# A four-layer graph network on one Trainium2 core: weights loaded ahead, split operands kept per tile, first messages inside the last convolution chunk, result loads together

## The chip, the core and the metric

The kernel runs on one core of a Trainium2 chip. The core has a matrix engine (TensorE, PE in the profile, with its weight loads listed as PEld), a vector engine (VectorE, DVE), an activation engine (ScalarE, ACT), a general engine (GpSimd, POOL) and a queue engine that mostly issues transfers (SyncE, SP). Each engine works through its own queue in order, and an instruction waits on semaphores for what other engines or transfers must have done. The sixteen DMA engines are shared by all queues. The metric is the device time of one execution in microseconds (us), taken as the median of three runs.

## The reference, cut to what matters

There are 8 graphs of 2048 nodes with 64 features and one adjacency matrix `adj` of 2048 x 2048 (zeros and ones, mostly zeros). Four layers follow each other, each in the form x = x + layer(relu(layernorm(x))). The change touches the end of layer 0, layers 1 and 2, and the end of layer 3.

```python
# layer 1, h = relu(layernorm(x)), K = 3 terms, D = 16 embedding dimensions
w = einsum('nd,dkio->nkio', embedding, weight);  b = embedding @ bias
x_g = [h, A @ h, 2 * A @ (A @ h) - h]
x = x + einsum('bnki,nkio->bno', x_g, w) + b
# layer 2, v = relu(layernorm(x)) with node 0 set to intervention_value
for _ in range(3):
    v = relu(concat(v, A @ v) @ W1.T + b1) @ W2.T + b2
x = x + v
# layer 3: attention of each node over its neighbours
x = x + softmax(adj * leaky_relu(e_src + e_dst)) @ (h @ weight) + bias
```

## The kernel before

**Layout.** Activations are kept as four pairs of graphs: for pair q a tile has 128 partitions (2 graphs x 64 features) and 2048 columns (nodes). Work along the nodes runs in four chunks of 512 columns (`ch`), or sixteen tiles of 128 nodes (`t` or `m`). Products with `adj` need the operand with the nodes on the partitions. Most large buffers are ten slots, `q0` to `q9`, of 16 KB per partition each, which the layers use again under other names.

**Product with the adjacency.** `adj_product` (L289) runs over the chunks, and in each over the sixteen tiles m. L300 loads a piece of `adj` transposed on SP (two tiles, 512 KB, with step=2), L312 rounds each tile on ACT to the reduced-precision format that the fast matmul takes, and eight matmuls follow (L153, all matmuls carry this line): four pairs times two halves of the operand, into `pp0` to `pp3`. To keep precision the operand is split into a rounded part `hi` (ACT, L219) and a rest `lo` (DVE, L220). `Split` holds these as four big buffers, `q6` to `q9`, each with eight node tiles. `first` runs ahead of a chunk's product, `after` behind each tile m, `done` at the chunk's end.

**End of layer 0.** `mix` (L608) works on the residual of layer 0 chunk by chunk, with its buffers `mix0` to `mix2` and `tanh` in `q6` to `q9`; with the norm it writes the operand of layer 1 (L618).

**Layer 1** (L1238). `by_node` transposes all node tiles (L1252) and splits them into `h_n`; a first product gives A h, and each chunk is transposed back into `ah`. Then `ah` is split into `ah_n`, the weights `wk` are loaded in six transfers (L1288, L1292) and adjusted by three DVE operations (L1295, L1296), the bias comes in two (L1300), and a second product runs. At the end of each of its chunks, `done2` loads the embedding (L1334, two transfers of 1 MB) and the residual (L1344), and runs the convolution: for each pair, four groups of eight matmuls into PSUM banks `pk`, sixteen multiplications (DVE, L1373), fourteen additions (POOL, L1378), and a fold (`po`, L1321). [...] The folds and the chunk's norm are put in a list, `waiting`, that `some` pops one at a time, during the next pair or the next chunk's product.

**Layer 2** (L1396). Three small weights are loaded (`block_diag`, L171 and L173) and combined by a few matmuls (`w2n`, `later`, `b1`). `messages(0, ...)` multiplies v by a weight for all sixteen tiles (`pn`), copies the result to `u`, and `u` is split into `u_n`. Three steps follow, each with one product; the chunk's own part is put into `pp` first (four matmuls). During the first steps `neighbours` finds, on POOL and DVE, the neighbours of each node for layer 3.

**Layer 3** gathers rows of neighbours on POOL (L1991), sums them and scatters the result to `att_rows` in DRAM (L2002). `result` (L2173) ends the kernel: for each chunk it loads x (L2178), for each of four tiles loads `att_rows` (L2182), transposes (L2185), adds (DVE, L2187), and stores four pieces (L2191), all transfers on SP.

**Order.** The program is recorded in the order of the source; a scheduler then sets the order in each engine's queue, within the dependences. A pool laid on memory that another pool has left waits for that memory tile by tile.

Of the kernel before, what the change touches and what calls it, by code (L numbers as in the profile page):

```python
# [7 lines left out]
F = mybir.dt.float32  # L8
# [11 lines left out]
P = 128  # L20
# [85 lines left out]
class Split:  # L106


    def __init__(self, slots, name, tags=("q6", "q7", "q8", "q9")):
        self.hi = Halves(slots, f"{name}_hi", tags[:2], True)  # L110
        self.lo = Halves(slots, f"{name}_lo", tags[2:], True)
        self.parts = self.hi, self.lo


class Kernel:
# [173 lines left out]
    def adj_product(self, src, w, ps, done, each=None, first=None, after=None, bufs=4, step=2):  # L289

        nc = self.nc
        for ch in range(NC):
            out = [ps.tile([P, CW], F, name=f"pp{q}", tag=f"pp{q}") for q in range(NP)]
            if first is not None:
                first(ch, out)
            for g in range(NT // step):
                at = w.tile([P, step, CW], F, name="adj_t", bufs=bufs)
                nc.sync.dma_start(  # L300
                    at,
                    self.a["adjT"][g * step * P : (g + 1) * step * P, ch * CW : (ch + 1) * CW]
                    .rearrange("(t p) n -> p t n", p=P),
                )
                for i in range(step):
                    m = g * step + i
                    if each is not None:
                        each(ch, m, at[:, i])
                    moving = at[:, i]
                    if self.short:  # L310
                        moving = w.tile([P, CW], F12, name="adj_12", bufs=bufs)
                        nc.scalar.copy(moving, at[:, i])  # L312
                    for j, part in enumerate(src.parts):
                        for q in range(NP):
                            self.mm(
                                out[q], self.exact(part(m)[:, q * P : (q + 1) * P]),
                                moving,
                                start=first is None and m == 0 and j == 0,
                                stop=m == NT - 1 and j == 1,
                            )  # L320
                    if after is not None:
                        after(ch, m, moving)
            done(ch, out)
# [282 lines left out]
    def mix(self, slots, ind, g, fcw, av, each=None):  # L606
# [4 lines left out]
        ring = slots.tile([P, 4, 2, CW], F, name="tanh", tag="q9")  # L611
        xe, xo = self.chebyshev(slots)
# [8 lines left out]
        with (  # L621
# [9 lines left out]
            for ch in range(NC):  # L631
                s = slice(ch * CW, (ch + 1) * CW)
                x, sq, xr = (b[:, ch % 2] for b in big)
# [604 lines left out]
    def layer1(self, slots):  # L1238
        nc, tc, a = self.nc, self.tc, self.a
        xe, xo = self.chebyshev(slots)  # L1240
        h_n = Split(slots, "h_n")
        ah = Halves(slots, "ah", ("q4", "q5"), True)
        lo, hi = slice(0, D), slice(D, P)
        ident = self.ident

# [9 lines left out]
        with (  # L1255
# [17 lines left out]
            self.adj_product(h_n, w, ps, done)  # L1273
        ah_n = Split(slots, "ah_n")
# [3 lines left out]
        with (  # L1278
            tc.tile_pool(reuse_waits="tile", name="k1", bufs=1) as k,
# [3 lines left out]
            DO = DE * D  # L1283
            w01 = []
            for i, order in enumerate(((0, 1), (1, 0))):
                t = k.tile([P, DO], F, name=f"w01_{i}")
                for j, kk in enumerate(order):
                    nc.sync.dma_start(t[j * D : (j + 1) * D], a["wk"][kk])  # L1288
                w01.append(t)
            w2 = k.tile([P, DO], F, name="w2")  # L1290
            for j in range(2):
                nc.sync.dma_start(w2[j * D : (j + 1) * D], a["wk"][2])  # L1292

            for t, h in zip(w01, (lo, hi)):
                nc.vector.tensor_sub(t[h], t[h], w2[h])  # L1295
            nc.vector.tensor_scalar_mul(w2, w2, 2.0)  # L1296

            bias = k.tile([P, NBLK], F, name="bias")
            for j in range(2):
                nc.sync.dma_start(  # L1300
                    bias[j * D : (j + 1) * D],
                    a["bias1"].rearrange("(b j) o -> j o b", j=2)[j],
                )

            fold = k.tile([P, D], F, name="fold")
            nc.vector.tensor_add(fold, ident[:, lo], ident[:, hi])
# [21 lines left out]
            def done2(ch, out):  # L1328
                while waiting:
                    some()  # L1330
                s = slice(ch * CW, (ch + 1) * CW)
# [16 lines left out]
                for q in range(NP):  # L1348
# [32 lines left out]
                    waiting.append(lambda q=q, accs=accs: fold_up(x, q, accs))  # L1381
# [9 lines left out]
            self.adj_product(ah_n, w, ps, done2, after=some, bufs=3)  # L1391
            while waiting:
                some()


    def layer2(self, slots):  # L1396
# [4 lines left out]
        with (  # L1401
# [5 lines left out]
            w1v = self.block_diag(k, a["W1T"][:D], "w1v")  # L1407
            w1e = self.block_diag(k, a["W1T"][D:], "w1e")
            w2 = self.block_diag(k, a["W2T"], "w2")

            w2n = k.tile([P, P], F, name="w2n")
            pw = ps2.tile([P, NP, P], F, name="pn")
            nc.tensor.transpose(pw[:, 0], w2, self.ident)
            nc.vector.tensor_copy(w2n, pw[:, 0])
            pw = ps2.tile([P, NP, P], F, name="pn")
            self.mm(pw[:, 0], w2n, w1v)
            self.mm(pw[:, 1], w2n, w1e)
            self.mm(pw[:, 2], self.col("b2").to_broadcast([P, P]), w1e)
            self.mm(pw[:, 3, :1], w1v, self.col("b2"))
            later = k.tile([P, 3, P], F, name="later")  # L1420
            nc.vector.tensor_copy(later, pw[:, :3])
            b1 = k.tile([P, 1], F, name="b1")
            nc.vector.tensor_add(b1, pw[:, 3, :1], self.col("b1"))
            own = [w1v, later[:, 0], later[:, 0]]
            seen = [w1e, later[:, 1], later[:, 1]]
            bias = [self.col("b1"), b1, b1]
            full = [P, NP, P]
            for q in range(NP):
                nc.vector.tensor_copy(v(q)[:, 0:1], self.col("iv"))

            def messages(step, tiles):

                for t in tiles:
# [4 lines left out]
                    if step == 0:  # L1438
                        self.copy(to, pn)
                    else:  # L1440
                        nc.vector.tensor_add(to, pn, later[:, 2].unsqueeze(1).to_broadcast(full))
# [12 lines left out]
            messages(0, range(NT))  # L1454
            for step in range(3):
# [3 lines left out]
                u_n = Split(slots, "u_n")  # L1459
                for t in range(NT):  # L1460
                    self.split(u_n, t, u(t))
# [88 lines left out]
    def layer3_near(self, slots):  # L1550
# [6 lines left out]
        with (  # L1557
# [8 lines left out]
            for _ in range(12):  # L1566
                next(first)
            for part in others:
# [299 lines left out]

class Scores:
# [73 lines left out]
class Near:  # L1943
# [5 lines left out]
    def __init__(self, kern, slots, w, ps):  # L1949
# [4 lines left out]
        self.x = slots.tile([P, 2, NP, CW], F, name="x_end", tag="q2")  # L1954
# [218 lines left out]
    def result(self):  # L2173

        nc, w, kern = self.nc, self.w, self.kern
        for ch in range(NC):
            x = self.x[:, ch % 2]
            nc.sync.dma_start(x, kern.xs[3][ch])  # L2178
            for i in range(TC):
                t = ch * TC + i  # L2180
                r = self.att(t)
                nc.sync.dma_start(r, kern.att_rows[t * P : (t + 1) * P])  # L2182
# [7 lines left out]
            for q in range(NP):  # L2190
                nc.sync.dma_start(kern.a["out"][q, :, ch * CW : (ch + 1) * CW], x[:, q])  # L2191


def kernel(tc, a):
    with ExitStack() as ctx:
        kern = Kernel(tc, ctx, a)
        with (
# [11 lines left out]
            def rest(short):  # L2209
                kern.short = short  # L2210
                with tc.tile_pool(reuse_waits="tile", name=f"taken{int(short)}", bufs=1) as slots.pool:
# [4 lines left out]
                    kern.layer1(slots)  # L2216
                    kern.layer2(slots)
# [71 lines left out]
```

## Time and profile before

| | |
|---|---|
| time, median of three runs | 2193.83 us (2192.85 to 2193.92) |
| the profiled execution's own time | 2206.33 us |
| its span, first to last instruction | 2204.5 us |
| PE busy | 1961.8 us, 89% of the span |
| DVE busy | 1135.3 us, 52% |
| ACT, POOL busy | 713.0 and 709.2 us, 32% each |
| bytes moved by DMA | 253.66 MB, mean 115 GB/s |
| loads of `adj` transposed, 512 KB each | 160, 4.0 us median from issue to landing |
| loads of `adj` transposed, 256 KB each | 64, 3.1 us |
| embedding, residual of layer 1 (1 MB each) | 11.8 us, 4.9 us |

Times in the profile are us from the span's start. A record of the timeline gives start, busy time, engine, line, operation, output and input, the number of records, and in brackets how long the engine was idle before and what released it. A float32 matmul leaves two records for one instruction; those of the products leave one.

### The profile page before, as it was taken

To read this page: it belongs to the slowest core of one execution; us is meant where nothing else is said; L and a number is where in the kernel's file an instruction comes from. 1 tells how busy PE (TensorE), PEld (TensorE's weight loads), DVE (VectorE), ACT (ScalarE), POOL (GpSimd) and SP (SyncE) were. 2 spreads that over 40 slices of the span, in tenths; PEclk is the share of its full clock that TensorE was granted. 3 is DMA by queue.
4 is the path that set the end of the run, shared out by engine and by line. 5 is a ranking of instruction groups with operands and counts; after the bars stand their busy time and mean duration, and the time that the engine had idled before them with its cause. 6 is when DMAs were issued, how large, how long until landed. Compare 5 with 4: busy or idle time off the path is not lost.

```text
span 2204.5 us, 21222 instructions
## 1 busy us (share of the span) xinstructions
PE 1961.8 (89%) x7461; PEld 1166.3 (53%) x7466; DVE 1135.3 (52%) x1964; ACT 713.0 (32%) x1351; POOL 709.2 (32%) x595
## 2 busy tenths in 40 slices
PE   5869999978879979999999998999999999679883
PEld 1426766632237755353443533777777666345432
DVE  7877677725651133525434245898602222349772
ACT  6422555524543341020110201434334333257300
POOL 0000467754310004707447173011000000278760
PEclk8868999977759989999999998999999999789986
DMA  8230233431124361050220402356433443465655
GB/s 317 75 107 22 90 112 115 129 129 57 39 77 120 118 159 53 0 153 1 76 77 10 106 1 77 118 192 219 154 123 124 144 144 125 143 189 169 185 152 203
DMA packets 108286, 253.66 MB, mean 115 GB/s; under 512 B 20400, under 2 KB 20544, under 8 KB 100864
## 3 DMA queue, kind: packets, MB, share of 16 engines
q1 hardware_dynamic: 91056, 185.64, 26.7%
q0 software_dynamic: 17104, 66.47, 9.9%
q8 instruction: 63, 1.03, 0.2%
q14 instruction: 63, 0.52, 0.1%
HBM read 218.30 MB, written 33.78 MB: 114 GB/s over the span
## 4 chain that ended last, share of the span: by engine, by line
PE 55%; DVE 11%; POOL 7%; issue 6%; DMA 5%; ACT 3%; SPq 1%; POOLq 0%; DVEq 0%; ACTq 0%
PE pp L153 23%; PE pk L153 16%; PE bank L153 4%; PE acc L153 3%; POOL ring L1991 2%; PE p L153 2%; PE pn L153 2%; DMA q<-in_adj_dram,order 1%; POOL q L1826 1%; DVE q L1841 1%; POOL dt L644 1%; DVE top L1532 1%; PE pd L153 1%; PE po L153 1%; PE pt L1252 1%
## 5 line engine op out<-in xcount | busy, mean ns | idle before, releaser
L312 ACT CAST adj<-adj_t 128x512 fp32r<-128x512 f32 x384 | 236.9, 619 | 724.2 <-PE pp L153 633.6
L1378 POOL TENSOR_TENSOR acc<-acc,y 128x512 f32<-128x512 f32 x224 | 277.4, 1269 | 451.7 <-DVE y L1373 451.7
L153 PE MATMUL pk<-q,w 128*128 128x512 f32 (+1 forms) x1024 | 358.1, 612 | 12.7 <-DVE w L1295 11.7
L153 PEld LDWEIGHTS pk<-q,w 128*128 128x128 f32 (+1 forms) x1024 | 136.6, 188 | 230.3 <-issue 182.5
L153 PE MATMUL acc<-q,ident 128*128 128x512 f32 x416 | 206.3, 623 | 28.9 <-DVE q L2081 17.1
L1373 DVE SCALAR_TENSOR_TENSOR y<-pk,bias,q 128x512 f32<-128x512 f32 x224 | 157.7, 746 | 138.0 <-PE pk L153 128.1
L153 PE MATMUL pp<-adj,u_n_hi 128*128 128x512 f32 x768 | 217.6, 402 | 0.0
L153 PE MATMUL pp<-adj,u_n_lo 128*128 128x512 f32 x768 | 214.7, 399 | 0.0
L153 PEld LDWEIGHTS pp<-adj,u_n_hi 128*128 128x128 f32 x768 | 143.9, 189 | 38.6 <-issue 5.4
L153 PEld LDWEIGHTS pp<-adj,u_n_lo 128*128 128x128 f32 x768 | 145.1, 189 | 34.8
L1991 POOL DMA_INDIRECT ring<-f_rows,near x121 | 140.2, 1159 | 67.9 <-issue 28.0
L153 PEld LDWEIGHTS acc<-q,ident 128*128 128x128 f32 x416 | 77.8, 197 | 106.6 <-issue 50.9
L2095 POOL IOTA q<- 128x2048 int32 x1 | 1.8, 1836 | 318.6 <-PE p L153 318.6
L1373 DVE SCALAR_TENSOR_TENSOR acc<-pk,bias,q 128x512 f32<-128x512 f32 x32 | 22.6, 746 | 144.9 <-PE pk L153 144.9
L153 PE MATMUL pp<-adj,x_ind_hi 128*128 128x512 f32 x256 | 94.7, 486 | 2.2 <-DVE q L722 1.9
L1826 POOL TENSOR_TENSOR q<-q,beta 128x512 f32<-128x512 f32 x57 | 68.0, 1194 | 54.5 <-DVE beta L1802 30.8
L153 PE MATMUL bank<-std,from_rows 32*128 32x512 f32 x128 | 47.5, 936 | 41.9 <-DVE std L260 33.8
L153 PE MATMUL pp<-adj,h_n_hi 128*128 128x512 f32 x256 | 79.4, 423 | 0.0
L1518 POOL DMA_INDIRECT q<-in_adj_dram,order x15 | 21.9, 1459 | 174.9 <-DVE top L1532 136.0
L153 PE MATMUL pp<-adj,h_n_lo 128*128 128x512 f32 x256 | 76.7, 413 | 0.0
L2062 DVE TENSOR_TENSOR q<-ring,e 128x1024 f32<-128x1024 f32 x58 | 70.1, 1220 | 11.5 <-PE acc L153 11.3
L153 PE MATMUL pp<-adj,ah_n_hi 128*128 128x512 f32 x256 | 73.8, 408 | 0.8 <-ACT adj L312 0.8
(416 smaller groups left out, 3179.0 us busy)
## 6 DMA issues: line engine op xcount, KB each, us to landing
adj_t<-in_adjT_dram SPq DMA_DIRECT2D x160, 512.0 KB, 4.0
rows<-in_adj_dram SPq DMA_DIRECT2D x16, 1024.0 KB, 5.5
adj_t<-in_adjT_dram SPq DMA_DIRECT2D x64, 256.0 KB, 3.1
q<-x SPq DMA_DIRECT2D x12, 1024.0 KB, 4.9
q<-in_embT_dram SPq DMA_DIRECT2D x8, 1024.0 KB, 11.8
x<-q SPq DMA_DIRECT2D x8, 1024.0 KB, 3.8
x_ch<-in_xT_dram SPq DMA_DIRECT2D x4, 1024.0 KB, 6.1
h_rows<-q SPq DMA_DIRECT2D x16, 256.0 KB, 3.6
```

Of the source, the lines that this page charges most:

```text
L153: self.nc.tensor.matmul(out, lhsT, rhs, start=start, stop=stop)
L312: nc.scalar.copy(moving, at[:, i])
L644: nc.gpsimd.tensor_sub(dt, th[0], th[1])
L1252: nc.tensor.transpose(pt[:, q], src(q)[h, s], ident[h, h])
L1373: nc.vector.scalar_tensor_tensor(y, pks[b, half], bias[:, b : b + 1], emb[:, b], op0=OP.add, op1=OP.mult,)
L1378: nc.gpsimd.tensor_add(acc, acc, y)
L1518: nc.gpsimd.indirect_dma_start(row, None, self.a["adj"], bass.IndirectOffsetOnAxis(ap=order[:, 1, t : t + 1], axis=0),)
L1532: nc.vector.max(out=eight, in_=row)
L1826: self.nc.gpsimd.tensor_tensor(x, x, by.unsqueeze(2).to_broadcast([P, NB, D]), op=OP.mult)
L1841: nc.vector.tensor_add(d, d, self.pas.pop(i - 1))
L1991: self.nc.gpsimd.indirect_dma_start(to, None, self.kern.f_rows[:], bass.IndirectOffsetOnAxis(ap=index, axis=0))
L2062: nc.vector.tensor_tensor(y.rearrange("n i (b f) -> n i b f", b=NB), block[:, i : i + 2, : NB * D].rearrange("n i (b f) -> n i b f", b=NB) ...
```

## The change

Four groups of edits:

1. **Split operands per tile.** A new class `Source` holds hi and lo as 32 tiles of their own, one for each node tile and half, in a pool that is opened once for layers 1 and 2. The last chunk of `mix` takes its x, square and norm buffers from `q4` and `q5`.
2. **Weights ahead.** Layer 1's weights, bias and `fold`, and layer 2's three weights (new class `Steps`), are loaded and adjusted at the start of layer 1, ahead of its first product. The first product then holds three buffers of `adj` in place of four; the second loads single tiles (step=1, five buffers, two for the rounded tiles).
3. **First messages.** Layer 2's combined weights are made at the start of the first convolution chunk. In the last chunk the messages of tiles 0 to 11 go into `waiting`; there one entry is popped after each of the four groups of a pair, not only after the second. The messages are split straight from PSUM, without `u`. Tiles 12 to 15 follow the last norm.
4. **Result.** All four x chunks are loaded near the start of layer 3 (two in a new buffer), the sixteen loads of `att_rows` are issued together, and the stores go out on ACT's queue.

```diff
+class Source:
+    def __init__(self, pool):
+        hi, lo = (
+            [pool.tile([P, NB * D], F, name=f"{name}{t}") for t in range(NT)]
+            for name in ("hi", "lo")
+        )
+        self.hi, self.lo = hi.__getitem__, lo.__getitem__
+        self.parts = self.hi, self.lo
...
-                        moving = w.tile([P, CW], F12, name="adj_12", bufs=bufs)
+                        moving = w.tile([P, CW], F12, name="adj_12", bufs=casts or bufs)
...
+        end = [slots.tile([P, 2, NP, CW], F, name=f"end{i}", tag=f"q{4 + i}") for i in range(2)]
+        end = end[0][:, 0], end[0][:, 1], end[1][:, 0]
...
-                x, sq, xr = (b[:, ch % 2] for b in big)
+                x, sq, xr = end if ch == NC - 1 else (b[:, ch % 2] for b in big)
...
-    def layer1(self, slots):
+    def layer1(self, slots, k2):
+        self.steps = Steps(self, k2)
+        with tc.tile_pool(reuse_waits="tile", name="k1", bufs=1) as k:
+            self.chebyshev_layer(slots, k)
...
-        h_n = Split(slots, "h_n")
+        h_n = self.source
...
-            self.adj_product(h_n, w, ps, done)
-        ah_n = Split(slots, "ah_n")
+            self.adj_product(h_n, w, ps, done, bufs=3)
+        ah_n = self.source
...
+                if ch == 0:
+                    steps.prepare(bank)
+                if ch == NC - 1:
+                    for t in range(NT - TC):
+                        waiting.append(
+                            lambda t=t: steps.first_messages(v, u_n, t, bank())
+                        )
...
                         if blk == 2:
                             some()
-                    waiting.append(lambda q=q, accs=accs: fold_up(x, q, accs))
+                        elif ch == NC - 1:
+                            some()
+                    waiting.insert(0, lambda q=q, accs=accs: fold_up(x, q, accs))
...
-            self.adj_product(ah_n, w, ps, done2, after=some, bufs=3)
+            self.adj_product(ah_n, w, ps, done2, after=some, bufs=5, step=1, casts=2)
             while waiting:
                 some()
+            for t in range(NT - TC, NT):
+                steps.first_messages(v, u_n, t, bank())
...
-            messages(0, range(NT))
...
-                u_n = Split(slots, "u_n")
-                for t in range(NT):
-                    self.split(u_n, t, u(t))
+                u_n = self.source
+                if step > 0:
+                    for t in range(NT):
+                        self.split(u_n, t, u(t))
...
+            for ch in range(NC):
+                tc.nc.sync.dma_start(near.x[ch], self.xs[3][ch])
...
+    def first_messages(self, v, u_n, t, bank):
+        if t == 0:
+            for q in range(NP):
+                self.nc.vector.tensor_copy(v(q)[:, 0:1], self.kern.col("iv"))
+        pn = bank.rearrange("n (q f) -> n q f", q=NP)
+        for q in range(NP):
+            self.kern.mm(pn[:, q], v(q)[:, t * P : (t + 1) * P], self.w1e)
+        self.kern.split(u_n, t, bank)
...
-        self.x = slots.tile([P, 2, NP, CW], F, name="x_end", tag="q2")
+        x = slots.tile([P, 2, NP, CW], F, name="x_end", tag="q2")
+        more = w.tile([P, 2, NP, CW], F, name="x_more")
+        self.x = [x[:, 0], x[:, 1], more[:, 0], more[:, 1]]
...
+        for t in range(NT):
+            nc.sync.dma_start(self.att(t), kern.att_rows[t * P : (t + 1) * P])
         for ch in range(NC):
-            x = self.x[:, ch % 2]
-            nc.sync.dma_start(x, kern.xs[3][ch])
+            x = self.x[ch]
...
-                nc.sync.dma_start(r, kern.att_rows[t * P : (t + 1) * P])
...
-                nc.sync.dma_start(kern.a["out"][q, :, ch * CW : (ch + 1) * CW], x[:, q])
+                nc.scalar.dma_start(kern.a["out"][q, :, ch * CW : (ch + 1) * CW], x[:, q])
```

## The prediction

> **What bounds the kernel now.** I read the page's first two tables, then the chain of waits in order of time, then each engine's timeline around the four places that the edits touch, then the table of stretches.
>
> ```profile
> PE 1961.8 (89%) x7461; PEld 1166.3 (53%) x7466; DVE 1135.3 (52%) x1964; ACT 713.0 (32%) x1351; POOL 709.2 (32%) x595
> ...
> PE   5869999978879979999999998999999999679883
> ```
>
> PE is the bound over most of the span: in layers 1 and 2 its slices stand at 9, so a matmul put there costs its full length. Time can come only from seams where PE sits idle or cold. The chain across the middle of layer 1 shows the largest:
>
> ```profile
> 793.25 15.11 DMA w<-in_wk_dram
> ...
> 808.44 1.23 DVE w L1295
> 809.67 0.09 issue
> 809.76 3.75 PE pk L153 x4
> 813.51 30.69 PE pp L153 x128
> 844.21 16.21 PE pk L153 x47
> ```
>
> The second product waits for the convolution's weights because two of its matmuls stand ahead of it in PE's queue. PE's records give the idle time, 11.65 us:
>
> ```profile
> 796.61 1.50 PE L1252 MATMUL pt<-ident,q 64*128 64x64 f32 x18 [0.27 <-DVE q L1267]
> 809.76 3.75 PE L153 MATMUL pk<-q,w 128*128 128x512 f32 x4 [11.65 <-DVE w L1295]
> 812.52 2.69 PE L153 MATMUL pp<-adj,ah_n_hi 128*128 128x512 f32 x4
> ```
>
> The stretches (length, busy us and count of PE, PEld, DVE, ACT, POOL, granted clock, DMA share, GB/s) of the change from layer 1 to 2, of a convolution chunk, and of the end:
>
> ```profile
> 1340.00:1365.00 25.00, 15.26 (x34) 3.92 (x30) 13.86 (x35) 4.62 (x8) 8.57 (x10) 0.72 0.38 132
> 1365.00:1388.00 23.00, 22.86 (x146) 19.96 (x147) 15.91 (x38) 13.82 (x25) 0.29 (x1) 0.86 0.15 47
> 845.00:934.00 89.00, 89.00 (x263) 33.26 (x261) 44.37 (x64) 1.11 (x3) 64.34 (x52) 1.00 0.01 4
> 2156.00:2204.50 48.50, 14.68 (x64) 10.80 (x64) 12.40 (x17) 0.00 (x0) 0.97 (x1) 0.61 0.63 225
> ```
>
> The first messages (second row) keep PE 22.86 of 23 us busy already, and a convolution chunk leaves PE no idle time at all (third row). At the end everything waits for transfers: PE works 14.68 of 48.5 us.
>
> **Layer 0 to 1 (edits 1 and 2).** Before, the transposes and 18 product matmuls share PE from 636.1 to 663.5 at a low clock (0.79 us a matmul), and the first chunk's product ends at 690.3. In the changed program's queue all 32 groups of transposes stand ahead of the product. They then run at DVE's pace: a `lo` half takes 0.355 us (1.42 for four at 638.3), 32 take 11.4. The three weight operations come in among the last: 2.59 + 0.69 = 3.3 us. DVE ends at 638.3 + 14.7 = 653.0; four PSUM buffers lie between, so PE reaches the product near 652. 128 matmuls at 0.2287 us (117 in 26.76 at 696.7) are 29.3, and the cold start costs 2.4 as before (107 took 26.84 where the warm rate makes 24.5): end 683.7, **6.6 us gained**. What hides the moved transfers: on SP the first load of `adj` stands behind eight weight and bias transfers, which took 7.40 + 3.34 + 7.05 us to issue in the middle of layer 1, and six small ones (4.2 us at 1347). From 621.9 that makes 643.9, plus 4.0 to landing and 0.6 for the rounding: 648.5, still 3.5 ahead of PE. If that cover fails, each us late is a us lost: ends -5 and +10.
>
> **Middle of layer 1 (edits 1 and 2).** Weights and their DVE work are gone. Next in line are the transposes (end 798.1), then the first `adj` tile: the embedding's 2 MB go ahead of it on SP near 780, land about 11.8 later at 792, the 256 KB then by 795 (3.1 us), rounding to 796; cover 2 us. With the product starting at 798.1, 128 matmuls at 30.69/128 = 0.24 end at 828.8, against 844.2: 15.4. Less the two `pk` matmuls that had been done already (1.4) and the preparation of layer 2's weights, moved here (0.45 + 0.63 + 0.64 + 0.63 + 0.42 at 1365 to 1369, overlapping, about 2.5): **11.5 gained** (7 to 14).
>
> **Single tiles in the second product (edit 2).** Here the Trainium skill speaks against the change: "DMA: Bandwidth & Descriptors", section "Bandwidth", wants transfers of 1 MiB or more, and its fit in "Anatomy of one DMA" is 2 us fixed plus bytes at 436 GB/s. An estimate from it: 2.6 us for 256 KB. If loads did not overlap, each tile would take 2.6 in place of the 1.87 that eight matmuls need (two records of four in 813 to 844), over 64 tiles 47 us lost. The row for 256 KB says 3.1 us to landing, so no faster alone, but loads do overlap: with five buffers a load is asked for some 8 us ahead, and a stretch of this product moved 170 GB/s where 256 KB per 1.87 us is 140. I take the row: nothing. In the second chunk two loads behind the embedding are late in the trace (0.84 and 1.02 us of idle PE near 975 and 981); in the new order all of that chunk's loads stand ahead of the second embedding transfer: **1.9 gained** (-3 to 2). Two rounded tiles instead of three still leave ACT one tile (1.87) ahead against 0.62 for a rounding: nothing.
>
> **Layer 1 to 2 (edit 3).** After the norm (1363.7, last v written 1365.0) only four messages remain: eight records of 0.117 us each (3.73 for 32), 0.93, so 3.7; the own part, four at 1.03 plus 1 cold, 5.1; a small product 0.5. Full products start at 1374.4; before they started at 1388.3 with four done (0.9): 13.0 gained. But the twelve others now run inside the last convolution chunk, where PE has no gap: 12 x 0.93 = 11.2 us back. The folds are popped one group earlier, when POOL is not quite done (additions end about 6 us after the group's matmuls, the next group lasts 5.55): three waits of 0.5, 1.5. Queued behind those folds on PE is the next group. The banks suffice: a message's bank is needed again when both it and the older `pk` have been read. ACT is idle there, DVE half. Net **0.3** (-6 to +6). Had PE had gaps in the convolution, it would have been 12. Steps 2 and 3: PE is within 0.4 us of full at those seams; per-tile splits, nothing. The search for neighbours starts earlier with the products, not faster: nothing.
>
> **End (edit 4).** The last scatter lands at 2159.6 as before. Sixteen loads issued back to back need 7 us of SP at 0.43; loads and stores are 8.4 MB, and stretches of this end carry 367 to 420 GB/s when full, so 21 to 23 us for all. PE at its cold rate needs 3.87/4 = 0.97 us per tile, 15.5 from the first landing (2162.3): last tile near 2178, 2179 with shared transfers. From the last DVE operation (2193.7) to the span's end it took 10.8; so about 2190 to 2191.5: **13 gained** (8 to 16). The two x loads that move to layer 3's start (2 MB, 5.5 us at 380 GB/s) stand ahead of the first gathers. POOL issues those back to back every 1.25 us without waiting for landing, so most is absorbed: **-1** (-5 to 0).
>
> **Sum.** 6.6 + 11.5 + 1.9 + 0.3 + 13 - 1 = 32.3 us. The profiled execution took 2206.33 us around a span of 2204.5; it becomes 2174.0. The median, 12.5 below it, takes the same difference: 2193.83 - 32.3 = **2161.5 us**.
>
> **Rivals.** *Seam of layers 1 and 2 pays in full*: the convolution takes the messages in gaps that the matmul records, whose ends are modelled, hide. For: busy 89 of 89 is a modelled figure. Against: DVE and POOL show idle time waiting for PE. Another 12 us: 2149.5. *Cover fails*: weights, bias or embedding reach into the products, and the end is held by shared DMA: 6.6 lost, 5 of the 11.5, 5 of the 13: 2178. For: the bias transfers took 3.5 us each to issue. Against: the covers above. *Single-tile loads decide (slower)*: the product waits for each load as by the page's fixed cost. The place is the 64 tiles of the second product; it decides once a tile costs over 1.87 + 32.3/64 = 2.37 us; at 2.6 it gives 2161.5 + 47 = 2208.5. Against: 256 KB loads in flight together in the product of layer 0. *No change*: the scheduler puts the freed work back behind other waits, 2193.8. Against: the new queue orders.
>
> **Chances.** Forecast 0.64, full seam 0.12, cover fails 0.17, no change 0.03, slower 0.04. A measurement of this kernel can tell about 0.2%, 4.4 us, from no change. The range takes in forecast, full seam and cover: 2145 to 2181. Faster 0.93, same 0.03, slower 0.04.
>
> **What would show it.** The 11.65 us of idle PE ahead of `pk` are gone and the second product starts within 3 us of the last transpose; the first chunk's product ends 5 to 8 us earlier; the last convolution chunk is 11 to 14 longer while the gap behind it is some 13 shorter; the last store is issued near 13 us sooner after the last scatter. I would be wrong if PE waits for ACT's rounding in each tile of the second product, if the first product waits for its loads, or if layer 3's first products come 5 us later.

## The result, and the profile after

The changed kernel took **2164.41 us** (median of 4 runs, 2159.16 to 2172.28), the kernel before 2193.88 (2192.85 to 2198.31): a ratio of 0.9865 with an interval of 0.9829 to 0.9900, 29.5 us less. Measured again in five runs it took 2163.39 us, a ratio of 0.9861 (0.9835 to 0.9887). The forecast of 2161.5 holds.

The first two rows of the changed kernel's page (line numbers are now those of the changed kernel):

```profile
PE 1945.0 (90%) x7466; PEld 1163.0 (54%) x7466; DVE 1133.9 (53%) x1956; ACT 712.2 (33%) x1343; POOL 706.0 (33%) x595
...
PE   5879999978879999999999998899999999669885
```

PE does the same work (7466 instructions for 7461; matmul records can be missing) in a span of 2159.8 us for 2204.5. The profiled executions differ by 44.7 us, the medians by 29.5: the profiled execution of the kernel before was 12.5 us above its own median. So I don't read the gain from this pair alone. Layer 0's last store, for one, is issued at 621.6 in it, and between 613.8 and 618.4 in four variants below whose layer 0 is the same.

PE's timeline in the middle of layer 1, where before it sat idle for 11.65 us:

```profile
783.83 0.92 PE L1299 MATMUL pt<-ident,q 64*128 64x64 f32 x6 [0.27 <-DVE q L1314]
785.98 0.74 PE L1299 MATMUL pt<-ident,q 64*128 64x64 f32 x12 [1.24 <-ACT q L172]
786.65 1.95 PE L166 MATMUL pp<-adj,hi 128*128 128x512 f32 x4
...
818.16 0.27 PE L1898 MATMUL bank<-ident,w 128*128 128x128 f32 x1
818.30 1.13 PE L166 MATMUL pk<-q,w 128*128 128x512 f32 x2
819.26 0.38 PE L166 MATMUL bank<-w1v,w2n 128*128 128x128 f32 x2
819.48 0.39 PE L166 MATMUL bank<-w1e,w2n 128*128 128x128 f32 x2
819.71 0.39 PE L166 MATMUL bank<-w1e,cols 128*128 128x128 f32 x2
819.93 0.28 PE L166 MATMUL bank<-cols,w1v 128*128 128x1 f32 x2
820.07 3.45 PE L166 MATMUL pk<-q,w 128*128 128x512 f32 x8
```

The second product now follows the last transpose at once. What is late next is the 1.24 us in the second row: PE waits for a copy on ACT, and ACT had itself stood 2.37 us waiting for the first `adj` tile to land. The five small products of layer 2's weights (818.16 to 820.07) are the preparation that was moved here.

The traces of all kernels that ran can be cut at the same marks. The table gives lengths in us; the marks, in order, are the issue of layer 0's last store, the end of the first product's first chunk (the start of the transposes behind it), the last transpose, the start of chunk 0's last fold, the start of the last convolution chunk, the first own part of step 1 in layer 2, the first gather of layer 3, its last scatter, and the span's end.

| stretch | before | after | after, again |
|---|---|---|---|
| A: last store to chunk 0's product end | 69.4 | 63.2 | 63.6 |
| B: to the last transpose | 107.1 | 105.5 | 108.8 |
| C: second product, chunk 0's convolution | 139.9 | 128.3 | 128.1 |
| D: chunks 1 and 2, to the last one's start | 311.4 | 318.3 | 318.8 |
| E: last chunk, seam, step 0 | 290.7 | 281.1 | 281.3 |
| F: steps 1 and 2, to the first gather | 371.6 | 368.9 | 368.1 |
| G: first gather to last scatter | 245.0 | 239.6 | 240.3 |
| H: last scatter to the end | 47.7 | 36.9 | 35.1 |

A, C, E and H got shorter, D got **longer**. B and F stay within what two executions of one kernel differ by. G needs more traces.

### The profile page after: what moved, and what is told of

The parts are those of the page before. It is cut to its first block, busy times and chain, and to the rows that moved or that the text cites. A ratio compares the mean times of both kernels' runs of the same rounds, so it can differ in the third digit from the quotient of the medians.

```text
span 2159.8 us, 21301 instructions
## 1 busy us (share of the span) xinstructions
PE 1945.0 (90%) x7466; PEld 1163.0 (54%) x7466; DVE 1133.9 (53%) x1956; ACT 712.2 (33%) x1343; POOL 706.0 (33%) x595
## 3 DMA queue, kind: packets, MB, share of 16 engines
q8 instruction: 62, 1.02, 0.2%
## 5 line engine op out<-in xcount | busy, mean ns | idle before, releaser
L166 PE MATMUL pp<-adj,hi 128*128 128x512 f32 x1280 | 365.6, 405 | 0.1
L166 PE MATMUL pp<-adj,lo 128*128 128x512 f32 x1280 | 358.7, 400 | 0.0
L166 PEld LDWEIGHTS pp<-adj,hi 128*128 128x128 f32 x1280 | 242.1, 191 | 72.4 <-issue 16.0
L166 PEld LDWEIGHTS pp<-adj,lo 128*128 128x128 f32 x1280 | 244.0, 191 | 56.5
L166 PE MATMUL pp<-adj,x_ind_lo 128*128 128x512 f32 x256 | 71.7, 399 | 0.0
L166 PEld LDWEIGHTS pp<-adj,x_ind_hi 128*128 128x128 f32 x256 | 48.5, 189 | 38.9 <-issue 23.7
L1495 DVE SCALAR_TENSOR_TENSOR q<-p,cols,q 128x512 f32<-128x512 f32 x16 | 12.0, 751 | 108.4 <-PE p L166 107.5
## 6 DMA issues: line engine op xcount, KB each, us to landing
q<-in_embT_dram SPq DMA_DIRECT2D x8, 1024.0 KB, 11.5
```

Source lines behind the costliest of these rows:

```text
L166: self.nc.tensor.matmul(out, lhsT, rhs, start=start, stop=stop)
L1495: nc.vector.scalar_tensor_tensor(x[:, q], p2, self.col("b2"), x[:, q], op0=OP.add, op1=OP.add)
```

## The experiments

Twelve runs followed. Names with b_ start from the kernel before, names with a_ from the changed one.

**The changed kernel again** (no edit).

> The changed kernel once more, for a second trace of it. What belongs to the change must come again: end of the first product's chunk near 680, second product from near 787, stalls of 1 to 2 us ahead of pk in chunks 1 and 2, last convolution chunk of 104 us, first messages' own part near 1364. What is only scatter between executions may not: the 5.4 us by which layer 3 (first gather to last scatter) was shorter, 239.6 for 245.0, and the convolution chunks 1 and 2 that were 5.8 us longer than their stalls explain. If scatter: layer 3 is over 2 us off 239.6. If the change's: within 1 us of it. Time 2159 to 2172.

2163.39 us. G came again within 1 us and D too, so by what was written down they would belong to the change. That holds for D; G is taken up below.

**The end alone**, in the kernel before:

```
+            for ch in range(NC):
+                tc.nc.sync.dma_start(near.x[ch], self.xs[3][ch])
...
+        for t in range(NT):
+            nc.sync.dma_start(self.att(t), kern.att_rows[t * P : (t + 1) * P])
...
-                nc.sync.dma_start(kern.a["out"][q, :, ch * CW : (ch + 1) * CW], x[:, q])
+                nc.scalar.dma_start(kern.a["out"][q, :, ch * CW : (ch + 1) * CW], x[:, q])
```

> The kernel before with the edit of the end alone (four x tiles loaded at layer 3's start, the 16 loads of att_rows issued together, stores from ACT's queue). My sum: 13 less at the end and 1 lost at layer 3's start, so 2193.9 - 12 = 2182. By the trace of the changed kernel the end itself gave 10.9 (last scatter to the span's end 36.9 for 47.8): 2183 to 2184. Rival (shared DMA holds the end): 8 or less, 2186. Second rival: the end's edit also shortens layer 3 by 5: 2178.

2182.45 us, ratio 0.9951 (0.9938 to 0.9965): 11.4 us less by the medians. H is 34.8. The forecast's price for this edit, 13 less 1, stands.

**The x tiles alone**, in the kernel before; att_rows still loaded tile by tile, stores on SP.

```
+        more = w.tile([P, 2, NP, CW], F, name="x_more")
+        self.x = [x[:, 0], x[:, 1], more[:, 0], more[:, 1]]
...
-            x = self.x[:, ch % 2]
-            nc.sync.dma_start(x, kern.xs[3][ch])
+            x = self.x[ch]
```

> The kernel before with the end's x tiles alone: all four loaded at layer 3's start into buffers of their own; att_rows still loaded tile by tile and stored from SP as before. The whole edit of the end took 11 from the stretch behind the last scatter (46 to 48 -> 35), and in the seven traces that have it the first gather to the last scatter of layer 3 took 239.4 to 243.7, in the three without it 245.0 to 245.3. If the x tiles bring the end's gain (2 MB less to carry there): end stretch 40 to 42, time 2187; if the loads issued together and ACT's stores bring it: 45 to 47, 2193. If the x tiles shorten layer 3: 240 to 242; if not: 245.

Ratio 0.9966 (0.9952 to 0.9981) on a chip on which the kernel before took 2212.39. H is 39.2. In the kernel before, two x loads stand between the loads of att_rows on SP, behind the first eight stores:

```profile
2173.89 0.33 SPq L2178 DMA_DIRECT2D q<-x  x1
...
2176.47 0.32 SPq L2178 DMA_DIRECT2D q<-x  x1
```

SP's timeline at the end of the kernel with the x tiles alone:

```profile
2156.83 4.87 SPq L2185 DMA_DIRECT2D q<-att_rows  x9
2164.86 5.44 SPq L2194 DMA_DIRECT2D out_dram<-q  x8
2170.35 3.57 SPq L2185 DMA_DIRECT2D q<-att_rows  x7
2178.80 6.42 SPq L2194 DMA_DIRECT2D out_dram<-x_more  x8
```

Seven loads still stand behind eight stores on SP, and still 7 to 9 of the 11 us have gone (H is 46.0 to 47.8 in the five traces without any of this edit): most of the end's gain is the two x loads that are no longer in it. Loading together and storing from ACT bring the other 2 to 5 (H is 34.5 to 37.2 in the eight traces with all of it).

**Weights back at their old place**, in the changed kernel:

```
-        w01 = []
...
-        nc.vector.tensor_add(fold, ident[:, lo], ident[:, hi])
...
             tc.tile_pool(reuse_waits="tile", name="conv_ps", bufs=1, space=PSUM) as ps,
         ):
+            w01 = []
...
+            nc.vector.tensor_add(fold, ident[:, lo], ident[:, hi])
```

> The changed kernel with layer 1's weights, their DVE work and the bias loaded at their old place, between the first and the second product of layer 1. My sum on record: 11.5 lost in the middle (last transpose to the first fold's end of chunk 0: 128 -> 140), and the three weight operations leave the first seam, where they were priced at 3.3 of DVE's path: c. 0 to 3 gained there (63.3 -> 60 to 63): 2172 to 2175. Rival: single tiles and the new load order hide the weights even at the old place: 2163 to 2166.

2169.61 us, ratio 0.9886 (0.9867 to 0.9905), some 5 us slower than the changed kernel (the intervals overlap), but not where I had said. C stays at 128.1, A goes back to 69.2. The pool of the weights is still opened at the layer's start here, so their transfers find their place free and are issued during the first product (636.96 to 668.37) wherever their lines stand. In the kernel before, that pool is opened only after the first product's pools have closed, and the weights then stand on SP behind the embedding:

```profile
784.41 1.34 SPq L1334 DMA_DIRECT2D q<-in_embT_dram  x2
785.80 7.40 SPq L1288 DMA_DIRECT2D w<-in_wk_dram  x4
```

The embedding had waited 11.8 us for DVE's splits of `ah` (`ah_n_lo`, L220), whose slot `q4` it takes over. So the weights were late by the late pool and by their place behind a transfer that itself waited for its buffer; which of the two alone would have held them longer is not shown.

PE's timeline at the seam in this kernel:

```profile
634.24 1.35 PE L1274 MATMUL pt<-ident,q 64*128 64x64 f32 x12 [1.78 <-DVE lo L233]
635.52 0.79 PE L166 MATMUL pp<-adj,hi 128*128 128x512 f32 x1
636.24 0.69 PE L1274 MATMUL pt<-ident,q 64*128 64x64 f32 x4
636.86 0.79 PE L166 MATMUL pp<-adj,hi 128*128 128x512 f32 x1
637.58 0.70 PE L1274 MATMUL pt<-ident,q 64*128 64x64 f32 x8
```

The first `adj` load stands ahead of the weights on SP, and single product matmuls at 0.79 us each are in PE's queue between the transposes. In the changed kernel:

```profile
635.48 10.39 PE L1299 MATMUL pt<-ident,q 64*128 64x64 f32 x100 [1.78 <-DVE lo L233]
646.64 0.69 PE L1299 MATMUL pt<-ident,q 64*128 64x64 f32 x4 [0.77 <-DVE lo L233]
648.35 0.69 PE L1299 MATMUL pt<-ident,q 64*128 64x64 f32 x4 [1.02 <-DVE lo L233]
649.28 0.69 PE L1299 MATMUL pt<-ident,q 64*128 64x64 f32 x4 [0.25 <-DVE lo L233]
650.01 2.07 PE L166 MATMUL pp<-adj,hi 128*128 128x512 f32 x4
```

All transposes come first, with waits for DVE, and the product begins at 650.

**The weights ahead alone**, in the kernel before: the lines moved to the layer's start, with their pool.

```
     def layer1(self, slots):
+        with self.tc.tile_pool(reuse_waits="tile", name="k1", bufs=1) as k:
+            self.chebyshev_layer(slots, k)
...
+        DO = DE * D
+        w01 = []
...
-            self.adj_product(h_n, w, ps, done)
+            self.adj_product(h_n, w, ps, done, bufs=3)
...
-            tc.tile_pool(reuse_waits="tile", name="k1", bufs=1) as k,
...
-            DO = DE * D
-            w01 = []
```

> The kernel before with layer 1's weights and bias in a pool that is opened at the layer's start and loaded ahead of the first product (three load buffers there for four), nothing else; split buffers, messages, load sizes and the end as before. If the place of the weights' transfers ahead of the first adj loads is what puts the transposes ahead of the product, and the pool's early opening is what ends the wait in the middle, this alone gives both of the largest terms: from layer 0's last store to the first chunk's end 69 -> 63, from the last transpose to chunk 0's last fold 140 -> 127, 18 us in all, a ratio near 0.992 to the kernel before. Rival: the seam also needs the per-tile split buffers: 69 stays, 12 us, a ratio near 0.9945.

2183.08 us, ratio 0.9948 (0.9932 to 0.9964). C is 128.1: the 11.65 us are gone by this alone. A is 66.3, half of its gain. A goes with the number of product matmuls that stand ahead of the last transpose: 18 in the kernel before (A 69.4), 17 with the weights at their old place (69.2), 5 here (66.3), none in the changed kernel (63.2). In the changed kernel the three small weights of layer 2 go ahead too, and the first `adj` load is issued 10.3 us behind the last store, 6.6 here. Whether they or the per-tile buffers bring the other half of A's gain, no run separates.

**Per-tile split buffers alone**, in the kernel before, with the last mixing chunk's own slots.

```
-        h_n = Split(slots, "h_n")
+        h_n = self.source
...
-        ah_n = Split(slots, "ah_n")
+        ah_n = self.source
...
-                u_n = Split(slots, "u_n")
+                u_n = self.source
```

> The kernel before with the split buffers kept per tile, and the last mixing chunk in slots of its own; weights, messages, loads and the end as before. My sum on record: the seam from layer 0 to 1 alone, 6.6, so 2187; the stretch from the last store of layer 0 to the first product chunk's end 69.1 -> about 63. Rival from the traces: the 6.5 us by which step 0 of layer 2 was shorter (145 for 150 to 152) come from the per-tile buffers too (splits of one tile can be spread over the last product chunk): step 0 145, 2181. Against it: step 0 is shorter because the first messages are split straight out of PSUM without a copy: step 0 stays 150 to 152, 2187.

2189.01 us, ratio 0.9973 (0.9961 to 0.9984). None of the three theories: A stays at 68.9 with 18 matmuls between the transposes, C gets 3.5 shorter (the wait ahead of `pk` is 8.11 us), E about 2. C's part fits the queue above: with buffers of their own the splits of `ah` come earlier, the embedding waits 7.0 us for them in place of 11.8, and the weights behind it are issued 16.3 us ahead of the last transpose's end in place of 12.3.

**First messages split straight out of PSUM**, added to the last one:

```
                     if step == 0:
-                        self.copy(to, pn)
+                        self.split(self.source, t, pn.rearrange("n q f -> n (q f)"))
```

> The kernel before with per-tile split buffers, and the first messages split straight out of PSUM instead of copied and then split; all of them behind the norm as before. Step 0 of layer 2 took 150.4 to 152.2 before, 149.5 with per-tile buffers alone, 144.6 to 147.5 in the changed kernel and its variants. If the direct split is what shortened it: 145 to 147, and the time 2184 to 2186. If it is the earlier preparation of layer 2's weights or the other order of DVE's queue: 149 to 150, 2189.

Ratio 0.9946 (0.9925 to 0.9966), on the chip with 2212.39 before. E is 283.1, against 288.5 with the buffers alone and 290.7 before. Within step 0 PE waits for DVE ahead of the messages of step 1. These waits were 2.08 + 1.20 + 3.08 in the kernel before (and one of 2.59 just behind E's end), 2.28 + 0.93 + 2.49 with the buffers alone, and are 0.48 + 1.94 here: 3.3 of the 5.3 us. By these single traces this is the largest part of E's gain; the intervals of the two ratios overlap.

**No messages within the convolution**, in the changed kernel: all 16 behind the norm, the folds popped as before.

```
-                if ch == NC - 1:
-                    for t in range(NT - TC):
-                        waiting.append(
-                            lambda t=t: steps.first_messages(v, u_n, t, bank())
-                        )
...
-                        elif ch == NC - 1:
-                            some()
```

> The changed kernel with all 16 first messages behind the last norm instead of 12 of them inside the last convolution chunk, folds popped as before. My sum on record: net 0.3, so 2164.7. Rival, from the trace after: the last chunk gets 12.3 shorter, the gap behind it 16.7 longer, and step 0 stays as it is: 2169. Second rival: the 7.5 us by which step 0 was shorter come from the messages too (less work for DVE at its start): 2176. Third: the convolution had gaps for them and the seam pays in full: 2176, but with the last chunk only a few us shorter.

2161.16 us, ratio 0.9860 (0.9834 to 0.9886), the same as the changed kernel; E is 281.8. **The move itself is worth nothing.** The changed kernel's last chunk shows why:

```profile
1233.31 5.51 PE L166 MATMUL pk<-q,w 128*128 128x512 f32 x16
1238.75 1.16 PE L166 MATMUL bank<-w1e,q 128*128 128x128 f32 x8
1239.74 5.52 PE L166 MATMUL pk<-q,w 128*128 128x512 f32 x16
```

The group holds PE from 1233.31 to 1238.75, the message from there to 1239.74: it pushes the next group back by its 0.99 us, and twelve of them are 11.9.

**Single tiles alone**, in the kernel before (with the parameter `casts`, as in the change):

```
-            self.adj_product(ah_n, w, ps, done2, after=some, bufs=3)
+            self.adj_product(ah_n, w, ps, done2, after=some, bufs=5, step=1, casts=2)
```

> The kernel before with single adj tiles of 256 KB (five load buffers, two rounded tiles) in layer 1's second product, nothing else. My sum: 0 for the tiles and 1.9 gained by earlier late loads, 2192. Rival from the trace after: the first rounding of the next chunk stands ahead of the copies of the product on ACT and waits for a load behind the embedding, so the stalls stay (3.0 for 1.9 us): 2194 to 2195. Rival on record (a load's fixed cost per tile, 0.73 us on 64 tiles): 2241.

2198.45 us, ratio 1.0021 (1.0009 to 1.0033): 4.6 us **slower**. D fits: 310.4 to 313.4 in the six traces with pairs of tiles, 314.1 to 318.8 in the six with single tiles whose copies stay on ACT. PE's idle time within D separates the two more sharply: 8.1 to 8.5 us with pairs, 9.4 to 14.2 with single tiles (11.3 here). The rule of the Trainium skill ("DMA: Bandwidth & Descriptors", section "Bandwidth") has the sign of this. The estimate of 47 us made from that page's fit (section "Anatomy of one DMA") is ten times what was measured; the page gives the fit for transfers issued from GpSimd, and these are issued on SP. SP's and then ACT's timeline of the changed kernel in chunk 1 show the mechanism:

```profile
934.81 0.61 SPq L1364 DMA_DIRECT2D q<-in_embT_dram  x1
936.75 8.18 SPq L313 DMA_DIRECT2D adj_t<-in_adjT_dram  x5
944.98 1.46 SPq L1364 DMA_DIRECT2D q<-in_embT_dram  x1
946.54 15.22 SPq L313 DMA_DIRECT2D adj_t<-in_adjT_dram  x7
```

```profile
958.32 0.62 ACT L325 CAST adj<-adj_t 128x512 fp32r<-128x512 f32 x1 [4.59 <-DMA adj_t<-in_adjT_dram]
958.85 2.04 ACT L1376 COPY q<-pp 128x512 f32<-128x512 f32 x4
```

The first half of the embedding (1 MB) stands ahead of this chunk's last five `adj` loads (936.75), the second half ahead of the next chunk's first seven (946.54). A tile behind the second takes up to 11.7 us to land. The rounding of the *next* chunk's first tile stands ahead of the copies of this chunk's product on ACT, waits 4.59 us for its load, and PE waits 1.92 us for the copies. The kernel before has this order too; PE's wait for the copies there:

```profile
981.12 19.06 PE L153 MATMUL pk<-q,w 128*128 128x512 f32 x53 [1.02 <-ACT q L1346]
```

**The copies on DVE**, in the changed kernel (L1376):

```
-                    nc.scalar.copy(aah[:, q], out[q])
+                    nc.vector.tensor_copy(aah[:, q], out[q])
```

> The changed kernel with the four copies of the second product's chunk (L1376) on DVE instead of ACT, where the first rounding of the next chunk stands ahead of them. If that order is what makes PE wait 1.0 to 2.0 us ahead of pk in chunks 1 and 2, those waits go and the stretch from the end of chunk 0 to the last chunk's start (318 in two traces of the changed kernel) gets 2 to 4 shorter: 2160. Rival: PE waits for late adj tiles anyway, the wait moves to the rounding or to the next chunk: no change, 2163.

2160.89 us, ratio 0.9832 (0.9810 to 0.9854). D is 311.1. The same place in this kernel, all engines:

```profile
958.44 2.48 DVE L1376 COPY q<-pp 128x512 f32<-128x512 f32 x4 [21.75 <-PE pp L166]
958.93 5.51 PE L166 MATMUL pk<-q,w 128*128 128x512 f32 x16
...
960.34 1.26 ACT L325 CAST adj<-adj_t 128x512 fp32r<-128x512 f32 x2 [4.21 <-DMA adj_t<-in_adjT_dram]
```

ACT still waits 4.21 us for the late tile, but nobody waits for ACT. The waits of 1.92 and 1.05 ahead of `pk` are gone. E was 288.7 in this trace, 7 more than in the two of the changed kernel, and the traces say where: for the same 1089 or 1090 matmuls PE was busy 273.9 us in place of 266.7 and 267.4, at a granted clock of 0.96 in place of 0.99 and 0.98. In the times the gain doesn't stand out of the intervals.

**Messages in PE's waits**, in the changed kernel without messages in the convolution:

```
-            while waiting:
-                some()
-
-            for t in range(NT):
-                steps.first_messages(v, u_n, t, bank())
+            messages(3)
+            some()
+            some()
+            messages(5)
+            some()
+            messages(NT - 8)
```

> The changed kernel with the first messages placed in the waits of PE behind the last convolution chunk: three ahead of the last fold (PE waited 2.8 for POOL there), five ahead of the last norm's second half (4.2 for the deviation), eight behind it; none within the convolution. Theory: a message costs 0.99 within the convolution, and 7.0 us of waits stand open, so against either of the two placements run so far 6 to 7 gained: 2155 to 2157. Rival: the messages' roundings on ACT and differences on DVE get in the way of the norm's own work, and only 0 to 2 is gained: 2160 to 2163.

**2155.62 us**, ratio 0.9816 (0.9800 to 0.9832); its slowest run, 2157.09, is below the fastest of the changed kernel. PE behind the last convolution chunk, first in the changed kernel:

```profile
1341.21 2.29 PE L166 MATMUL po<-acc,fold 128*64 128x512 f32 x4 [2.78 <-POOL acc L1408]
1343.43 2.84 PE L166 MATMUL bank<-q,center 128*128 128x512 f32 x6
1346.21 1.86 PE L166 MATMUL bank<-q,to_rows 128*32 128x512 f32 x8
1352.29 1.13 PE L166 MATMUL bank<-std,from_rows 32*128 32x512 f32 x6 [4.22 <-DVE std L273]
```

and in this one:

```profile
1327.57 2.05 PE L166 MATMUL bank<-w1e,q 128*128 128x128 f32 x16 [0.21 <-DVE y L1398]
1330.13 1.07 PE L166 MATMUL po<-acc,fold 128*64 128x512 f32 x2 [0.51 <-POOL acc L1403]
...
1337.81 2.94 PE L166 MATMUL bank<-w1e,q 128*128 128x128 f32 x24
1342.65 3.07 PE L166 MATMUL bank<-w1e,q 128*128 128x128 f32 x16 [1.90 <-DVE lo L233]
1345.65 3.61 PE L166 MATMUL bank<-std,from_rows 32*128 32x512 f32 x8
```

The messages stand where PE had waited 2.78 us for POOL's last sum and 4.22 for the deviation. What is left of the two waits is 0.51 + 0.15 and one of 1.90. E is 276.8, 4.3 and 4.6 less than in the changed kernel's two traces; the rest of the some 8 us by which the medians differ lies in stretches that this edit doesn't touch.

**Both improvements**, the edits of the last two kernels together:

> Both improvements together: the first messages in PE's waits behind the last convolution chunk, and the copies of the second product on DVE. The first gave 8 against the changed kernel, the second 2.5 of uncertain size. If they add: 2152 to 2154. If the copies' gain was scatter between executions: 2155 to 2157.

Ratio 0.9811 (0.9788 to 0.9835), on the chip with 2212.39 before; E 274.2, D 315.4. Not to be told from the messages alone. The waits ahead of `pk` are gone here too, and PE's idle time in D is 9.2 us in place of 14.2 with the messages alone, but PE was busy 306.2 us there in place of 302.1, at a granted clock of 0.98 in place of 1.00.

## Why the prediction held, and where its steps did not

**Seam of layers 0 and 1 (6.6).** Measured 5.8 and 6.2. The queue was as described: all transposes first, then the product 32.0 us behind the store (30.4 forecast). What brings that order was only partly right. The per-tile buffers (edit 1) do nothing for it by themselves (A 68.9), the weights ahead (edit 2) bring half by themselves (66.3), and the other half is not separated. The cover was mis-sized to the safe side: the eight weight and bias transfers took 4.8 us to issue in place of 17.8, so the first `adj` load was issued 10.3 us behind the last store, not 22.3.

**Middle of layer 1 (11.5).** Measured 11.6 and 11.9. The cover of 2 us for the first tile failed by about 1 us. That the wait hung on the pool's opening and on the embedding ahead of the weights, not on the place of their lines, I had not seen.

**Single tiles (nothing, +1.9).** This step failed: it cost 4.6 us alone. The sentence that all of chunk 2's loads would stand ahead of the second embedding transfer came true, as it did before the change, but it does not help. The next chunk's first loads stand behind that transfer, and the copies stand behind the rounding of the first of them on ACT; that was not priced at all. Of the two waits put down to late loads, the second (1.02 us near 981) was already PE's wait for these copies. In the changed kernel D grew by 6.9 and 7.4, and not by waits alone. PE's idle time in it grew from 8.1 us to 9.4 and 13.6; for the same matmuls PE was busy 308.9 us in one trace and 305.3 in the other, with 303.3 before, at a granted clock of 0.97, 0.99 and 0.99.

**Layer 1 to 2 (net 0.3).** For the move of the messages this is what the runs show: the last chunk grew by 12.3 (12.7 forecast: 11.2 and 1.5), the stretch from its last `pk` to the second tile of layer 2's first product is 32.0 with the move and 45.6 without it (13.6, with 13.0 forecast), and undoing the move changed nothing. But E as a whole gained 9.4 and 9.6. The step that failed is "per-tile splits, nothing", with the reading that PE is within 0.4 us of full at the seams: PE stood 6.4 us in step 0 before, in the waits quoted above. The longest of them, with DVE's queue ahead of it, in the kernel before:

```profile
1495.16 2.35 DVE L1522 SCALAR_TENSOR_TENSOR q<-q,own,q 128x2048 f32<-128x2048 f32 x1 [5.38 <-DMA q<-in_adj_dram,order]
...
1502.02 2.29 DVE L1532 MAX8 top<-q 128x8 f32<-128x2048 f32 x1
1504.23 1.27 DVE L1441 TENSOR_TENSOR q<-pn,later 128x512 f32<-128x512 f32 x2
...
1504.95 3.55 PE L153 MATMUL pn<-later,q 128*128 128x128 f32 x16 [3.08 <-DVE q L1441]
```

DVE was not short of time here: it had just waited 5.38 us for a row that the neighbour search gathers. The addition that PE needs (L1441) stands behind four operations of the search. The sum had no term for the direct split, which takes a copy off DVE and ACT; with it E is 5.3 us shorter, and 3.3 of that is in these waits. Why they get shorter is not shown. Of E's whole gain, 7.2 and 6.5 us show as shorter busy time of PE (273.9 to 266.7 and 267.4), with the preparation gone from there and a granted clock of 0.99 and 0.98 in place of 0.96.

**End (13, less 1).** Measured 10.8 and 12.7 in H; the first gather was not later, so the -1 is 0. The size of the loads' term was off: SP took 16.40 us to issue the sixteen loads, not 7 (and 8.4 MB at 420 GB/s are 20 us, not 21). Here is SP's row, and then the row of H in the changed kernel (length; busy us and count of PE, PEld, DVE, ACT, POOL; granted clock, DMA share, GB/s). It shows that PE, with 15.45 us of work, was not the limit, and the DMA engines, busy for 0.68 of it on average, came nearer:

```profile
2125.79 16.40 SPq L2234 DMA_DIRECT2D q<-att_rows  x16
...
2122.90:2159.80 36.90, 15.45 (x64) 11.15 (x64) 11.92 (x16) 0.00 (x0) 0.97 (x1) 0.57 0.68 239
```

**The sum.** From the runs' ratios come buffers 5.9, direct split 5.9 further, end 10.7 and single tiles -4.6; from the traces come A's order 6.2 and the rest of C 8.1 (136.4 with the buffers to 128.3). Together that is 32.2, with several us of uncertainty, against 29.5 measured and 32.3 forecast. That the number came so near is partly luck: two errors, 6.5 too much at the single tiles and some 9 too little from layer 1 to 2, nearly cancelled. Of the rivals, the full seam falls (the messages cost 0.99 us each), a failing cover is seen only as 1 us, the single tiles were a loss but a small one, and no change lies outside the interval.

**Open.** G was 239.4 to 241.9 in six and 243.7 in one trace with the x tiles, 245.0 to 245.3 in three without, which looked like an effect of theirs; the kernel with the weights ahead alone, which has none, then gave 239.9. The cause was not found, and no gain is put down to it.

## What to carry to other kernels

A wait for a transfer is often a wait for a buffer, its own or that of a transfer ahead of it on the queue: ask which pool must close and what stands ahead, before moving the load's line. Work moved into a stretch where PE is full costs its length there; in the waits that the chain shows by name it fills time that is lost anyway. When a queue is re-ordered, read what stands ahead of the *late* instruction on each engine in order, since a rounding that waits for a load holds back every copy behind it.

## What the runs showed of the hardware

Matmuls scattered between small transposes stayed slow: with the weights at their old place each held PE for 0.72 us (635.52 to 636.24 above). Behind the last transpose of the changed kernel the first four took 1.87 together (650.01 to the next record at 651.88), and four took 0.98 soon after (653.59 to 654.57). The granted clock (third number from the end) is 0.50 over the mixed stretch, although PE is busy all of it, and 1.00 over most of the product in one piece:

```profile
634.24:658.30 24.06, 24.06 (x129) 14.62 (x129) 11.46 (x30) 11.36 (x31) 0.00 (x0) 0.50 0.40 114
...
655.00:681.26 26.26, 26.26 (x115) 21.22 (x113) 0.02 (x1) 9.31 (x16) 0.00 (x0) 1.00 0.48 141
```

The first row is of the kernel with the weights at their old place, the second of the changed one. Starting the product *later*, in one piece, ended it 6 us earlier.

The same two bias transfers took SP 7.05 us to issue behind 2 MB of embedding, 4.6 of which the trace puts down to a wait for the embedding to land, and 1.33 us with little in flight: what an issue takes can't be carried from one place to another without what is ahead of it.

On the chip where the kernel before took 2212.39 us, some 19 more than elsewhere, G was 253.2 to 257.3 in all three kernels traced there, 12 to 14 us more than in one kernel each with the same layer 3 on another chip (253.2 for 240.3, 254.2 for 240.4, 257.3 for 245.0), while C, E and H were as on the others. So most of what makes this chip slower lies in the stretch of layer 3's gathers; the rest was not found.
